# A message-passing layer on one core: loads between the parts of the tables, and gathers 8 to 13 that wait in half groups

## The chip, the cores and the metric

The kernel runs on one core of one Trainium2 chip. The metric is the device time in microseconds of one execution. Every time of a profile comes from one profiled execution and is counted from the start of its span, from the first to the last instruction.

## The reference, cut to what matters

A graph has 6250 nodes of 128 features and 100000 edges, sorted by destination. An edge's message is a small network of its source, its destination and four attributes; messages are summed by destination; a second network and two layer norms finish each node.

```python
src, dst = edge_index[0], edge_index[1]
msg_in = jnp.concatenate([node_features[src], node_features[dst], edge_features], axis=1)
h = jax.nn.silu(msg_in @ mW1 + mb1)
messages = h @ mW2 + mb2
aggregated = jax.ops.segment_sum(messages, dst, num_segments=N)
upd_in = jnp.concatenate([node_features, aggregated], axis=1)
u = jax.nn.silu(upd_in @ uW1 + ub1)
updated = u @ uW2 + ub2
return layer_norm(node_features + updated, ln_g, ln_b)
# and outside: x = layernorm(x + that)
```

Everything is float32.

## The kernel before, in words

**Tables.** The first layer is split by its inputs. For every node the kernel computes x times the source part of mW1 (`tab_a`) and x times the destination part plus the bias (`tab_b`) and stores both in HBM. This goes in seven `parts` of up to eight tiles of 128 nodes: `turn_x` transposes x on TensorE one part ahead, a product of 256 columns makes both tables at once, ScalarE copies one half, VectorE adds the bias to the other, and SyncE (SP) stores both (lines 377 to 405). The products use three PSUM buffers called `wide`.

**Groups.** The edges are worked in 98 groups of 1024, eight tiles of 128. For each group GpSimd (POOL) gathers eight tiles of rows by source index, one indirect DMA a tile (`fetch`, line 278). Groups 0 to 4 (`RAW = 5`) gather from x itself, because the table is not there yet, and are transposed later (`turn_rows` for groups 0 to 3, `turn_late` for group 4); from group 5 on they gather from `tab_a`. There are six gather buffers, so group g also waits until group g − 6 has been used.

**The loop over groups.** In iteration g: `load(g + 4)` brings the window of 96 rows of `tab_b` (`mv`, five buffers) that the group's sorted destinations fall into, the transposed attributes, and for every fourth group the list of near destinations; `hidden(g)` adds the gathered rows on VectorE and applies Silu on ScalarE; `products(g + 2)` makes on TensorE the part of the hidden layer that comes from destinations and attributes, out of a 0/1 matrix (`node_matrix`); `edge_matrix(g + 1)` makes the matrix for the sums; `by_nodes(g)` sums the messages' hidden rows into destinations on TensorE; `add(g − 2)` adds them to `acc`. Finished ranges of nodes go through `node_batch`, in pieces between the groups. For groups 0 to 4 `products` also multiplies the transposed gathered rows by the weights, so it holds twice as many matmuls as for later groups. A float32 product of 128 columns stands in the trace as two matmul records and two weight loads.

**What sets the order.** The order on SP, TensorE, VectorE and ScalarE is the order of the program. POOL's queue is ordered by a scheduler, which can put a tile that has to wait behind others of its own or the next group. `fetch(g, *after)` takes instructions of TensorE as extra dependencies: with one, tile 0 waits for it; with two, tile 0 waits for the first and tile 4 for the second. `begun[g]` is the first matmul of `products(g)`, `summing[g]` the first of the sums of g. The line in the code that names the reason reads "TensorE keeps up with the gathers". From group 14 on (`CLOSE`), group g waits in halves for `begun[g]` and `summing[g - 2]`; groups 5 to 13 wait as a whole for `begun[g - 5]`:

```python
        ahead = g + AHEAD
        if CLOSE <= ahead < NG:
            fetch(ahead, begun[ahead], summing[g])
        elif RAW <= ahead < NG:
            fetch(ahead, begun[ahead - 5])
```

Between the tables and the loop stand the loads that the first groups need (lines 406 to 414): the attribute rows of the weights into `mv`, the first chunk of attributes and its transposed rows in HBM (`attributes`, `attribute_rows`), the near destinations of groups 0 to 3 (`destinations`), fourteen window bases into registers of SP and VectorE (`load_bases`), and the four `turn_rows`.

Of the kernel before, what the change touches and what calls it, by code (L numbers as in the profile page):

```python
# [24 lines left out]
def kernel(  # L25
# [40 lines left out]
    nc = tc.nc  # L66
    N, H = x.shape
# [6 lines left out]
    NG = -(-E // GE)  # L74
    assert NG <= P
    W = 96
    NW = NP + W
    K1 = W + ED
    RB = 14
    AHEAD = 2  # L80
    CLOSE = 14
    LEAD = 4
    RAW = 5
# [14 lines left out]
    def groups(n, g):  # L98
        return [(i, min(g, n - i)) for i in range(0, n, g)]


    TURNED = 4
# [20 lines left out]
    def wide():  # L123
        return tables_ps.tile([P, G, P], F32, name="wide")
# [47 lines left out]
    mv = [consts.tile([K1, H], F32, name=f"mv{k}") for k in range(NM)]  # L172
# [102 lines left out]
    def tiles_of(g):  # L275
        return min(G, -(-(E - g * GE) // P))

    def fetch(g, *after):

        rows[g] = gath.tile([P, G, H], F32, name="ga")  # L280
        for i in range(tiles_of(g)):
            ins = nc.gpsimd.indirect_dma_start(  # L282
                out=rows[g][:, i, :],
                out_offset=None,
                in_=x if g < RAW else tab_a[:, :],
                in_offset=bass.IndirectOffsetOnAxis(
                    ap=src_i[:, g, i : i + 1] if g else src_0[:, i : i + 1], axis=0
                ),
            )
            part, at = divmod(i * len(after), G)  # L290
            if after and at == 0:
                tc.add_manual_dep(
                    ins.ins,
                    after[part].ins.name,
                    mybir.DependencyInfo(
                        mybir.DependencyClass.Sync, mybir.DependencyReason.DATA
                    ),
                    reason="TensorE keeps up with the gathers",
                )
# [8 lines left out]
    def attributes(c):  # L308
        t = turn.tile([EQ, EJ * ED], F32, name="ea_l")
        chunk = edge_attr[c * EC : (c + 1) * EC]  # L310
        nc.sync.dma_start(t, chunk.rearrange("(q j) d -> q (j d)", q=EQ))
        ea_l[c] = t

    def attribute_rows(c):
        t = turn.tile([EQ, ED, EJ], F32, name="ea_t")
        nc.scalar.copy(t, ea_l.pop(c).rearrange("q (j d) -> q d j", d=ED))
        rows = ea_d[:, c * EC : (c + 1) * EC]
        nc.sync.dma_start(rows.rearrange("d (q j) -> q d j", q=EQ), t)

    def destinations(g):  # L320

        n = min(NQ, NG - g)
        t = work.tile([W, NQ, GE], U8, name="near")
        flat = near_d[g : g + n].rearrange("(o g) e -> o (g e)", o=1)
        nc.sync.dma_start(
            t[:, :n].rearrange("w g e -> w (g e)"), flat.to_broadcast([W, n * GE])
        )
        for k in range(n):
            near[g + k] = t[:, k, :]
# [4 lines left out]
    def by_node(t):  # L334
        return t[:NP].rearrange("(i p) f -> p i f", p=P)
# [5 lines left out]
    def turn_x(i0, n):  # L341
        pt = wide()
        for i in range(n):
            ins = nc.tensor.transpose(pt[:, i, :], x_sb[:, i0 + i, :], ident)  # L344
        nc.scalar.copy(xT[:, i0 * P : (i0 + n) * P], pt[:, :n, :].rearrange("p i f -> p (i f)"))
        return ins

    def load_bases(g):
        _, vals = nc.values_load_multi_w_load_instructions(
            base_i[0:1, g : g + RB],  # L350
            engines=(ENG.SP, ENG.DVE),
            min_val=0,
            max_val=NP,
            skip_runtime_bounds_check_because=IN_RANGE,
        )
        for k, v in enumerate(vals):
            bases[g + k] = v
# [4 lines left out]
    def turn_rows(g):  # L362

        px = wide()
        for i in range(G):
            nc.tensor.transpose(px[:, i, :], rows[g][:, i, :], ident)
        nc.vector.tensor_copy(rows[g], px)
# [9 lines left out]
    for k, (i0, n) in enumerate(parts):  # L377
        if k + 1 < len(parts):
            turn_x(*parts[k + 1])

        tb = x_sb[:, i0 : i0 + n, :]
        ta = tpool.tile([P, G, H], F32, name="t", bufs=2)
        for j0, m in groups(n, G // 2):
            pm = wide().rearrange("p (i s) f -> p i s f", s=2)
            for j in range(m):
                cols = slice((i0 + j0 + j) * P, (i0 + j0 + j + 1) * P)
                ins = nc.tensor.matmul(pm[:, j], xT[:, cols], w1, start=True, stop=True)  # L387
            own = slice(j0, j0 + m)
            nc.scalar.copy(ta[:, own], pm[:, :m, 0, :])
            nc.vector.tensor_add(  # L390
                tb[:, own], pm[:, :m, 1, :], b1[:, None, :].to_broadcast([P, m, H])
            )
        nc.sync.dma_start(by_node(tab_a)[:, i0 : i0 + n, :], ta[:, :n])
        nc.sync.dma_start(by_node(tab_b)[:, i0 : i0 + n, :], tb)
        table.append(ins)
        if k == 1:
            fetch(2, *table)
        if k == 2:
            destination_lists()
        if k == 3:  # L400
            fetch(3, *table[2:])
        cols = slice(i0 * P, NW if i0 + n == NT else (i0 + n) * P)
        nc.vector.memset(acc[:, cols], 0.0)
        if k == 4:
            fetch(4, table[4])
    for t in mv:
        nc.sync.dma_start(t[W:], mW1[2 * H :])
    attributes(0)
    attribute_rows(0)
    destinations(0)  # L410
    load_bases(0)
    for g in range(TURNED):
        turn_rows(g)
    if E < NG * GE:
        pad = tpool.tile([ED, NG * GE - E], F32, name="pad")
# [6 lines left out]
    def rows_ps():  # L422
        return ps.tile([P, G, P], F32, name="pre")

    def node_y():
        return node_ps.tile([P, BT, H], F32, name="y")
# [173 lines left out]
    def edge_matrix(g):  # L600

        oh = work.tile([P, G, W], F32, name="oh", bufs=3)
        nc.vector.tensor_tensor(  # L603
            oh,
            w_row[:, None, :].to_broadcast([P, G, W]),
            rel[:, g, :, None].to_broadcast([P, G, W]),
            op=OP.is_equal,
        )
        return oh

    begun, summing = {}, {}

    def products(g):
        pre = rows_ps()
        st = stbuf[g % NST].rearrange("k (i c) -> k i c", i=G)
        for i in range(tiles_of(g)):
            ins = nc.tensor.matmul(pre[:, i, :], st[:, i, :], mv[g % NM], start=True, stop=g >= RAW)  # L617
            begun.setdefault(g, ins)
            if g < RAW:
                nc.tensor.matmul(  # L620
                    pre[:, i, :], rows[g][:, i, :], w1[:, 0, :], start=False, stop=True
                )
        return pre
# [26 lines left out]
    def by_nodes(g, h, oh):  # L650

        pt = degrees(g)
        sums(g, pt, h, oh, 0, tiles_of(g))
        return pt
# [13 lines left out]
        node_matrix(g)  # L668
    oh, h, pt, running = {0: edge_matrix(0)}, {}, {}, []
    pre = {g: products(g) for g in range(2)}  # L670
    for g in range(NG):
        if g == 3:
            load_weights()
        if g == 4:
            destination_checks(node_y())
        if g == 5:
            fuse_weights()
        for c in range(1, NC):
            if g == max(1, c * EC // GE - 10):
                attributes(c)  # L680
            if g == max(1, c * EC // GE - 10) + 1:
                attribute_rows(c)
        if g + LEAD < NG:
            load(g + LEAD)
        last = g >= NG - 1
        if not last:
            h[g] = hidden(g)
        if TURNED <= g + 2 < RAW:
            turn_late(g + 2)
        if g + 2 < NG:  # L690
            pre[g + 2] = products(g + 2)
        if g + MADE < NG:
            node_matrix(g + MADE)
        if g + 1 < NG:
            oh[g + 1] = edge_matrix(g + 1)
        if g - 2 in pt:
            add(g - 2, pt.pop(g - 2))
        if last:
            break
        pt[g] = by_nodes(g, h.pop(g), oh.pop(g))  # L700
        ahead = g + AHEAD
        if CLOSE <= ahead < NG:
            fetch(ahead, begun[ahead], summing[g])
        elif RAW <= ahead < NG:
            fetch(ahead, begun[ahead - 5])
        if g >= NG - 3:
            add(g - 1, pt.pop(g - 1))
        for i0, n, first in batches[:-1]:
            if g == (first if first >= NG - 3 else first + 1):
                running.append(node_batch(i0, n, *node_tiles(nodes, node_y)))  # L710
        for _ in range(2 if g >= NG - 6 else 1):
            advance(running)

    g = NG - 1
# [194 lines left out]
```

## Time and profile before

| what | us |
|---|---|
| median of 3 runs | 1210.3 (1208.65 to 1211.81) |
| the profiled execution | 1208.8 |
| its span | 1207.0 |
| POOL busy | 740.8 (61%) |
| TensorE matmuls busy | 735.1 (61%) |
| VectorE busy | 488.3 (40%) |
| ScalarE busy | 244.6 (20%) |
| mean busy share of the DMA engines, by slice | 0.6 to 0.7 at the start, 0.1 to 0.3 in the loop |
| mean granted TensorE clock | 0.678 |

No engine is busy all the time. The busy time of POOL is that of issuing gathers; their data move on the DMA engines. The idle time of an engine is put down in the profile to what released it: another engine's line, a DMA, "issue" where no wait ended just before, or "remote" where the release could not be matched to an instruction.

### The profile page before, as it was taken

What the parts mean: (1) busy time and instruction counts of PE and PEld (TensorE: products, weight loads), DVE (VectorE), ACT (ScalarE), POOL (GpSimd) and SP (SyncE); (2) the same over time, 40 slices, a digit from 0 to 9 for tenths busy, and PEclk for the clock granted to TensorE, in tenths of its full rate; (3) what the DMA queues carried; (4) which work ended last, traced back from release to release, by engine and by line L of the source; (5) the groups of instructions that cost most, each with busy time, mean ns of one, the idle gap of its engine ahead of it and who ended that gap; (6) DMA issues with size and microseconds to landing.
All of it is one profiled execution on the core that took longest, in us unless ns stands there. A gap on an engine that the chain in (4) does not pass through costs nothing.

```text
span 1207.0 us, 11413 instructions
## 1 busy us (share of the span) xinstructions
PE 735.1 (61%) x3655; PEld 656.4 (54%) x3655; DVE 488.3 (40%) x1023; ACT 244.6 (20%) x306; POOL 740.8 (61%) x790
## 2 busy tenths in 40 slices
PE   4655366855666576556556556655575665485673
PEld 3545366745555465456446445554565654474562
DVE  3460253634325325326326326326236235235343
ACT  1211012312103202112112103102112211211224
POOL 7536554466666666666666666666666666566660
PEclk9777766876657666766666776676676567666666
DMA  7653121323222313222222223222322222222220
GB/s 186 177 158 89 41 56 39 85 60 80 72 52 79 78 50 84 55 74 72 82 58 71 76 57 77 73 54 74 79 57 76 63 69 74 57 69 65 54 53 24
DMA packets 70221, 88.96 MB, mean 74 GB/s; under 512 B 20719, under 2 KB 51838, under 8 KB 70154
## 3 DMA queue, kind: packets, MB, share of 16 engines
q0 software_dynamic: 25024, 51.30, 17.3%
q1 hardware_dynamic: 40552, 34.96, 10.0%
q10 hardware_dynamic: 4578, 1.89, 0.6%
q8 instruction: 31, 0.51, 0.2%
q14 instruction: 36, 0.29, 0.1%
HBM read 76.71 MB, written 11.38 MB: 73 GB/s over the span
## 4 chain that ended last, share of the span: by engine, by line
issue 40%; POOL 27%; another core or an unknown queue 10%; DVE 9%; PE 9%; DMA 3%; ACT 1%; SPq 1%; DVEq 0%; POOLq 0%; ACTq 0%
POOL ga L282 27%; PE pt L645 2%; PE pre L617 2%; PE wide L387 2%; DVE oh L603 2%; DVE s L633 1%; DVE st L590 1%; DMA ga<-tab_a,src_i 1%; DVE st L482 1%; DMA x_sb<-in_x_dram 1%; DVE y L526 1%; PE wide L344 1%; DVE mv L483 0%; DMA w<-in_L_gnn_mW_dram 0%
## 5 line engine op out<-in xcount | busy, mean ns | idle before, releaser
L282 POOL DMA_INDIRECT ga<-tab_a,src_i x742 | 701.7, 946 | 412.9 <-issue 209.8
L617 PE MATMUL pre<-mv,st 100*128 100x128 f32 x1564 | 318.2, 366 | 189.8 <-issue 150.6
L645 PE MATMUL pt<-oh,h 128*128 128x96 f32 x1564 | 305.9, 349 | 209.2 <-issue 200.1
L645 PEld LDWEIGHTS pt<-oh,h 128*128 128x128 f32 x1564 | 286.0, 266 | 229.1 <-issue 220.7
L617 PEld LDWEIGHTS pre<-mv,st 100*128 100x128 f32 x1564 | 288.8, 274 | 212.6 <-issue 179.8
L633 DVE TENSOR_TENSOR s<-ga,pre 128x1024 f32<-128x1024 f32 x92 | 112.2, 1220 | 426.9 <-DMA ga<-tab_a,src_i 207.9
L634 ACT ACTIVATE h<-s 128x1024 f32<-128x1024 f32 x92 | 97.0, 1056 | 655.6 <-issue 367.3
L590 DVE TENSOR_SCALAR_CACHE_REDUCE st<-near,p_next 96x1024 f32<-96x1024 uint8 x98 | 124.2, 1269 | 6.2 <-DMA near<-near_d 6.0
L603 DVE TENSOR_TENSOR oh<-w_row,rel 128x768 f32<-128x768 f32 x98 | 93.1, 950 | 27.1 <-remote 24.0
L526 DVE TENSOR_TENSOR y<-y,xs 128x512 f32<-128x512 f32 (+2 forms) x13 | 8.4, 648 | 130.5 <-issue 110.0
L282 POOL DMA_INDIRECT ga<-in_x_dram,src_i x32 | 30.3, 947 | 17.4 <-issue 8.2
L634 ACT ACT_TABLE_LOAD x25 | 32.1, 1283 | 15.7 <-PE pre L620 13.8
L488 ACT ACT_TABLE_LOAD x26 | 33.4, 1283 | 3.6 <-DVE mv L483 3.1
L387 PE MATMUL wide<-w,xT 128*128 128x256 f32 x98 | 26.8, 432 | 10.7 <-DVE x_sb L390 8.0
L513 ACT ACTIVATE uT<-y,ub_col 128x512 f32<-128x512 f32 (+2 forms) x13 | 8.4, 645 | 116.8 <-remote 90.1
L387 PEld LDWEIGHTS wide<-w,xT 128*128 128x128 f32 x98 | 21.1, 222 | 15.0 <-DVE x_sb L390 8.6
L524 PEld LDWEIGHTS y<-u,uT 128*128 128x128 f32 x94 | 22.2, 318 | 9.0 <-issue 8.9
L524 PE MATMUL y<-u,uT 128*128 128x128 f32 x94 | 25.4, 419 | 0.0
L663 DVE TENSOR_TENSOR deg<-deg,pt 1x96 f32 x98 | 24.4, 249 | 1.0
L658 DVE TENSOR_TENSOR acc<-acc,pt 128x96 f32 x98 | 23.7, 242 | 1.8 <-PE pt L645 1.7
L483 DVE BATCH_NORM_AGGREGATE mv<-st 128x2 f32<-128x6 f32 x98 | 17.8, 182 | 13.1 <-remote 5.1
L620 PE MATMUL pre<-w,ga 128*128 128x128 f32 x80 | 19.8, 332 | 2.2 <-issue 2.2
(122 smaller groups left out, 368.3 us busy)
## 6 DMA issues: line engine op xcount, KB each, us to landing
ga<-tab_a,src_i POOLq DMA_INDIRECT x742
near<-near_d SPq DMA_DIRECT2D x24, 384.0 KB
mv<-tab_b SPq DMA_DIRECT2D x98, 48.0 KB
tab_a<-t SPq DMA_DIRECT2D x6, 512.0 KB
tab_b<-x_sb SPq DMA_DIRECT2D x6, 512.0 KB
xs<-in_x_dram SPq DMA_DIRECT2D x11, 256.0 KB
out_dram<-z SPq DMA_DIRECT2D x11, 256.0 KB
st<-ea_d SPq DMA_DIRECT2D x98, 16.0 KB
```

What stands on the lines that cost most here:

```text
L282: ins = nc.gpsimd.indirect_dma_start(out=rows[g][:, i, :], out_offset=None, in_=x if g < RAW else tab_a[:, :], in_offset=bass.IndirectOffs ...
L387: ins = nc.tensor.matmul(pm[:, j], xT[:, cols], w1, start=True, stop=True)
L488: nc.scalar.activation(r[:, :n], mv[:, :n, 1], AF.Sqrt, bias=eps)
L524: nc.tensor.matmul(y[:, i, :], by_p[:, :, i], u2, start=False, stop=i == n - 1)
L590: nc.vector.tensor_scalar(stbuf[g % NST][:W], near.pop(g), p_next, 0.0, op0=OP.is_equal, op1=OP.add, accum_out=deg_q[g // DQ % 2][:, g % D ...
L603: nc.vector.tensor_tensor(oh, w_row[:, None, :].to_broadcast([P, G, W]), rel[:, g, :, None].to_broadcast([P, G, W]), op=OP.is_equal,)
L617: ins = nc.tensor.matmul(pre[:, i, :], st[:, i, :], mv[g % NM], start=True, stop=g >= RAW)
L633: nc.vector.tensor_add(s[:, :n], ga[:, :n], ps[:, :n])
L634: nc.scalar.activation(h[:, :n], s[:, :n], AF.Silu)
L645: ins = nc.tensor.matmul(pt[:, :W], h[:, i, :], oh[:, i, :], start=i == 0, stop=i == tiles_of(g) - 1)
L658: nc.vector.tensor_add(at, at, pt[:, :W])
L663: nc.vector.tensor_add(at, at, pt[row, W:])
```

## The change

Three things are done. The loads named above, and the turns of groups 0 and 1, are put between the parts of the tables: the attributes after part 0, the weights' rows after part 1, the transposed attribute rows and the first turn after part 3, the near destinations, the bases and the second turn after part 4. The gathers of groups 5 to 7 are issued before the loop and lose their wait for products. Groups 8 to 13 are then issued in every second iteration, from iteration 1 to 11, and each waits in two halves: group 8 for products 2 and 3, group 9 for 4 and 5, and so on to group 13 for 12 and 13. From group 14 on the waits are the same.

```diff
@@ -77,7 +77,6 @@
     RB = 14
-    AHEAD = 2
     CLOSE = 14
@@ -393,23 +392,26 @@
         table.append(ins)
+        if k == 0:
+            attributes(0)
         if k == 1:
             fetch(2, *table)
+            for t in mv:
+                nc.sync.dma_start(t[W:], mW1[2 * H :])
         if k == 2:
             destination_lists()
         if k == 3:
             fetch(3, *table[2:])
+            attribute_rows(0)
+            turn_rows(0)
         cols = slice(i0 * P, NW if i0 + n == NT else (i0 + n) * P)
         nc.vector.memset(acc[:, cols], 0.0)
         if k == 4:
             fetch(4, table[4])
-    for t in mv:
-        nc.sync.dma_start(t[W:], mW1[2 * H :])
-    attributes(0)
-    attribute_rows(0)
-    destinations(0)
-    load_bases(0)
-    for g in range(TURNED):
+            destinations(0)
+            load_bases(0)
+            turn_rows(1)
+    for g in range(2, TURNED):
         turn_rows(g)
@@ -668,6 +670,9 @@
     pre = {g: products(g) for g in range(2)}
+
+    for g in range(RAW, 8):
+        fetch(g)
     for g in range(NG):
@@ -698,11 +703,11 @@
         pt[g] = by_nodes(g, h.pop(g), oh.pop(g))
-        ahead = g + AHEAD
-        if CLOSE <= ahead < NG:
-            fetch(ahead, begun[ahead], summing[g])
-        elif RAW <= ahead < NG:
-            fetch(ahead, begun[ahead - 5])
+        if CLOSE <= g + 2 < NG:
+            fetch(g + 2, begun[g + 2], summing[g])
+        elif g % 2:
+            at = g // 2 + 8
+            fetch(at, begun[g + 1], begun[g + 2])
         if g >= NG - 3:
```

## The prediction

> **What bounds the kernel now.** First the page: POOL, which issues the gathers, has the costliest group.
>
> ```profile
> span 1207.0 us, 11413 instructions
> ...
> L282 POOL DMA_INDIRECT ga<-tab_a,src_i x742 | 701.7, 946 | 412.9 <-issue 209.8
> ```
>
> One gather is busy for 946 ns, and the timeline shows 0.30 us before the next one of an undisturbed run: 1.25 us each, 978 us for all 782. The other 229 us of the span are what must be understood. The waits of POOL (us in total, times, longest) say where they are:
>
> ```profile
> POOL ga L282 <- issue: 220.2, 680, 11.8
> POOL ga L282 <- remote: 138.7, 55, 4.0
> POOL ga L282 <- PE pre L617: 37.2, 8, 20.0
> POOL ga L282 <- DMA mv<-in_L_gnn_mW_dram: 10.5, 1, 10.5
> ```
>
> Most of "issue" is the 0.30 us. "Remote" is a wait of 2.5 to 4 us about every 16 gathers; by the built program nearly all of these are waits for TensorE, whose release was not matched. The long ones lie at the start. The timeline of POOL (start, us, what, idle before it), from the first gather of the new table to where the steady pattern begins:
>
> ```profile
> 71.33 0.94 POOL L282 DMA_INDIRECT ga<-tab_a,src_i  x1 [10.53 <-DMA mv<-in_L_gnn_mW_dram]
> ...
> 83.37 0.94 POOL L282 DMA_INDIRECT ga<-tab_a,src_i  x1 [3.61 <-PE pre L617]
> 88.23 0.94 POOL L282 DMA_INDIRECT ga<-tab_a,src_i  x1 [3.92 <-PE pre L617]
> ...
> 161.06 0.94 POOL L282 DMA_INDIRECT ga<-tab_a,src_i  x1 [11.76 <-issue]
> ...
> 221.19 0.94 POOL L282 DMA_INDIRECT ga<-tab_a,src_i  x1 [20.00 <-PE pre L617]
> ```
>
> The last line is the mark of this prediction, M: the first tile of group 14, which waits for the product of group 14. Before it lie 78 gathers of the table: 97.5 us of work in 149.9 us, so 52 us of pauses. After it POOL issues 664 gathers, at 1.44 us each, and the tail follows.
>
> Why is TensorE late? The stretches (busy us and number of PE, PEld, DVE, ACT, POOL; clock, DMA share, GB/s) show it working in fits:
>
> ```profile
> 82.00:96.00 14.00, 13.68 (x106) 13.71 (x107) 7.02 (x11) 4.31 (x4) 6.89 (x8) 0.85 0.38 101
> 96.00:111.00 15.00, 4.72 (x18) 3.94 (x18) 0.00 (x0) 0.10 (x1) 9.15 (x10) 0.63 0.35 77
> ...
> 119.00:131.00 12.00, 0.00 (x0) 0.00 (x0) 0.00 (x0) 0.33 (x1) 8.13 (x9) 0.69 0.22 56
> ...
> 174.00:184.00 10.00, 3.41 (x10) 2.40 (x11) 0.35 (x1) 0.28 (x2) 5.19 (x6) 0.71 0.17 44
> ...
> 204.00:221.00 17.00, 15.07 (x104) 14.70 (x104) 15.88 (x32) 10.53 (x11) 0.00 (x0) 0.75 0.25 68
> ```
>
> While POOL gathers without a break, TensorE runs fast for 90 to 140 records (weight loads and matmuls together, mostly 105 to 127), then drops to about one matmul a microsecond, until POOL pauses. Every slow stretch ends when POOL has stood still for about 2 us. Counted in the timeline, a pause of 2.0 us or more brings the fast pace back; pauses of 1.0 and 1.1 us (at 787.5 and 1111.2) did not. So POOL's pauses feed TensorE, and TensorE's lateness makes the pauses.
>
> **What the Trainium skill says.** "SBUF — State Buffer", Who interferes with whom, has PE share no port with GpSimd and only the DVE and GpSimd pair contend; so ports don't explain the slow stretches, which the trace shows all the same (18 matmuls in 15 us). "Runtime: NRT & Kernel Launch", Instruction fetch mechanics, calls fetching autonomous and mostly hidden, in blocks of 256 instructions; the 105 to 127 records fit no such block. I name no mechanism and use the measured pattern.
>
> **The change, part by part.** From 82.2 to 221.2 TensorE issued 532 matmuls in 139.0 us. Slow were 96–111, 119–131, 144–150, 174–184 and 195–204: 52 us with 50 matmuls. Outside them 482 matmuls took 87 us, 5.5 per us.
>
> *Loads moved (SP, ACT).* No transfer is added. Five loads of mv rows (1.79 us of issue at 68.96), attributes, their rows, near and the load of bases leave the stretch after the tables. In SP's queue they now stand ahead of later table stores, which could wait behind them. SP's gaps between stores are 3 to 9 us there, so I take nothing for the loads; the load of bases takes 1.55 us on SP and its engine DVE waits too. The moved ACT copy (1.08 us) falls in a gap of 2.3 us. If SP had no gap, the five loads and near would cost some 2.3 us.
>
> *First nodes turned earlier.* Two of the four turns (8 transposes, 1.1 us; one DVE copy, 1.16 us) go between the parts. DVE then holds 2.3 us of copies and about 1.8 us of base loading more before the last adds, in a part where it was busy for 5.0 of 7.3 us; TensorE's last products wait for the second copy's buffer. I take 1.9 us for the last store of tab_a: gathers begin at 73.2 instead of 71.33. Bounds: 0 and 4.1 us.
>
> *Start of the products.* Before: the pad is stored late (76.79, behind near and bases), near lands at about 80.2, first product 82.3. After: the last two copies end near 71.8, pad issues at 72.3, lands 2.9 us later as before (76.79 to 79.70), the st load goes at 75.2, and 2.6 us later (79.70 to 82.33 before) the first product starts: 77.8, so 4.5 us earlier.
>
> *New waits.* Gathers 5 to 7 lose the wait for products; 6 and 7 still wait for the buffers of groups 0 and 1 (six buffers). By the built order, from M on POOL's queue is identical. Before M, halves of groups 8 to 13 wait for products 2 to 13, two groups of TensorE (128 records) per eight gathers (10 us). The walk, with 108 fast records per pause of 2 us or more and 1.4 records per us when they are used up:
> - 73.2–83: group 5. Product 0 (64 records, 5.6 us) ends at 83.4; a pause of 0.5 us refills nothing.
> - 83.7–93.4: group 6. Product 1 runs dry at 86.5; slow for 10 us. Pause 3 us.
> - 96.5–116.2: groups 7 and 8. Slow from 104, 14 us. Pause 4 us.
> - From 120.5: waits at each half group. Pauses at about 129, 140 (6 us more behind the destination checks on DVE), 158, 171, 186 and 199, each ending about 2 us after the refill; slow for 12 us in all.
>
> Slow time is then 36 us by the walk; I take 34. With t for the whole ramp, 5.5 (t − 34) + 34 = 532 gives t = 124.5, so M lies at 77.8 + 124.5 = 202.3; POOL's own work needs 73.2 + 97.5 = 170.7 and 32 us of pauses remain, six to eight of 3 to 5 us, which agrees. M gains 18.9 us. All behind the gathers (DVE adds, sums, node batches) waits on the same queue; the cover of the moved waits is the lead of gathers, which at M is again one to two groups in both kernels.
>
> *Sum.* 1207.0 − 18.9 = 1188.1 of span. The profiled execution was 1208.8, 1.8 above its span: 1189.9. The median of runs, 1210.3, is 1.5 above that: 1191.4, call it 1192.
>
> **Rivals.**
> 1. *Only the earlier start counts.* Slow time stays at 52 us and TensorE's 139 us move as they are: M at 216.8, 4.4 us gained, 1206. For it: M waits for TensorE, whatever POOL does. Against: before, five unbroken bursts of 10 to 20 us made the slow time; after, only two of 20 us remain.
> 2. *Slower: the ramp takes the steady pace.* From 221.2 to 1165 TensorE did 2833 matmuls in 943.8 us, 3.0 per us, with POOL pausing only when caught. If freeing groups 5 to 7 and splitting the rest leave only pauses too short to refill, the ramp goes that way: 532 / 3.0 = 177 us, M at 255, 34 us lost, 1244. Halfway (3.4 per us) M is at 234, 1223. It decides against the change below 532 / 143.4 = 3.71 per us. For it: the 20.00 us pause, in which TensorE did 104 matmuls, goes. Against: two groups per eight gathers hold POOL back twice as often as the steady one.
> 3. *Bound by POOL.* Every wait finds TensorE ready after the least pause: 170.7 plus seven pauses of 2.5 us, M at 188, 33 us gained, 1177.
>
> **How the numbers follow.** Forecast 0.55, ending at 1180 to 1200 by slow time of 20 to 44 us; rival 1 has 0.15, rival 2 0.20, rival 3 0.10. A measurement tells about 0.3%, 3.6 us, from no change. Rival 1 lies at its edge: 0.06 of it counts as faster, 0.08 as same, 0.01 as slower. Faster 0.71, same 0.08, slower 0.21. The range must leave out 2 in 10: from 1176 (rival 3 in) to 1221 (the milder half of rival 2). The tables' 0 to 4.1 us and the loads' 2.3 us lie within it.
>
> **What would show it.** First gather from tab_a at 72 to 75; first product near 78, not 82; the eighth gather of group 5 no longer behind a pause; pauses of 3 to 5 us between 120 and 200 and none of 12 or 20; M near 202; from M to the end 986 us as before; "remote" waits about the same in number or a few more. Wrong: a first product after 82 (the tables were delayed by more than the loads saved), slow stretches above 52 us before M, or more than 3 us change behind M, where I claim nothing changes.

## The result, and the profile after

The changed kernel takes 1194.2 us (median of 4 runs, 1194.1 to 1194.9) against 1209.5 for the kernel before: a ratio of 0.987, interval 0.9855 to 0.989. The forecast was 1192. The kernel before takes either about 1026 or about 1210 us and stays with one of them through a sitting, and on one and the same chip both were seen; the result, and the prediction, belong to the second.

The page of the changed kernel shows the gathers costing as much work as before (701.8 us) and having 19 us less idle time ahead of them (393.7, not 412.9):

```profile
span 1192.3 us, 11417 instructions
...
L281 POOL DMA_INDIRECT ga<-tab_a,src_i x742 | 701.8, 946 | 393.7 <-issue 194.4
```

POOL's waits (us in total, times, longest) say which ones went. The 20.0 us wait for a product is gone, and the longest wait for one is now 5.4; "remote", the steady wait, is 132.1 us for 138.7. The wait for the table (the first line of the timeline below) is 11.5 us:

```profile
POOL ga L281 <- issue: 204.5, 670, 0.5
POOL ga L281 <- remote: 132.1, 48, 4.0
POOL ga L281 <- PE pre L619: 26.4, 10, 5.4
```

The timeline of POOL, from the first gather of the new table to M, the first tile of group 14 (start, us, what, idle before it):

```profile
74.81 0.94 POOL L281 DMA_INDIRECT ga<-tab_a,src_i  x1 [11.47 <-DMA tab_a<-t]
...
86.52 0.94 POOL L281 DMA_INDIRECT ga<-tab_a,src_i  x1 [2.03 <-remote]
...
131.85 0.94 POOL L281 DMA_INDIRECT ga<-tab_a,src_i  x1 [5.33 <-PE pre L619]
...
156.37 0.94 POOL L281 DMA_INDIRECT ga<-tab_a,src_i  x1 [5.47 <-DVE s L635]
...
204.54 0.94 POOL L281 DMA_INDIRECT ga<-tab_a,src_i  x1 [1.94 <-remote]
```

M lies at 204.54 instead of 221.19. The two pauses of 11.8 and 20.0 us ahead of it have become many of 2 to 5.5. The stretches of this ramp (busy us and number of PE, PEld, DVE, ACT, POOL; clock, DMA share, GB/s), from the first product to M, then the three in which TensorE does little, then everything behind M up to the last gathers:

```profile
77.10:204.50 127.40, 87.00 (x539) 81.16 (x540) 52.21 (x112) 25.72 (x33) 71.70 (x76) 0.73 0.27 72
96.00:109.00 13.00, 4.35 (x15) 3.03 (x13) 0.00 (x0) 0.00 (x0) 7.75 (x9) 0.62 0.29 76
115.00:129.00 14.00, 0.33 (x4) 0.09 (x1) 0.00 (x0) 1.02 (x1) 8.78 (x10) 0.67 0.23 57
142.00:148.00 6.00, 0.00 (x0) 0.00 (x0) 1.90 (x3) 0.00 (x0) 1.90 (x3) 0.63 0.13 33
204.50:1165.00 960.50, 581.96 (x2890) 521.81 (x2890) 389.79 (x820) 195.19 (x237) 628.20 (x664) 0.67 0.26 67
```

Slow time is 33 us (13 + 14 + 6) with 19 matmuls; it was 52 us with 50. From 156 on POOL pauses about every eight gathers and TensorE shows no long slow stretch. From M to the end it is 987.8 us, against 985.8 before.

Only the first of the three is TensorE at a slow pace: there its records come one by one, often 0.70 us apart (a matmul at 107.01, a weight load at 107.71, a matmul at 108.41). From 115 on it waits for VectorE, which has to copy four transposes before TensorE can go on, and that copy starts 14.0 us after their end (114.73 + 0.60):

```profile
114.73 0.60 PE L372 MATMUL y<-ident,ga 128*128 128x128 f32 x4
129.29 0.69 DVE L373 COPY ga<-y 128x512 f32<-128x512 f32 x1 [44.42 <-remote]
130.04 1.11 PE L372 MATMUL y<-ident,ga 128*128 128x128 f32 x4 [14.71 <-DVE ga L373]
```

The semaphore update that lets the copy go stands in the trace at 129.27. The ends of matmuls are modelled, so whether the transposes or only their signal came late is open. The third stretch is of the same kind: VectorE's destination checks begin at 146.10, 4.6 us after the matmul whose result they read (141.07 + 0.46), and TensorE waits for them. The kernel before has both at the same places (the copy at 132.37, 13.6 us after the transposes). So what comes late while POOL gathers is not TensorE's pace alone; it is also the handing over from TensorE to VectorE.

### The profile page after: what moved, and what is told of

It reads as the page before. It is cut to its first block, busy times and chain, and to the rows that moved or that the text cites. A ratio compares the mean times of both kernels' runs of the same rounds, so it can differ in the third digit from the quotient of the medians.

```text
span 1192.3 us, 11417 instructions
## 1 busy us (share of the span) xinstructions
PE 723.3 (61%) x3655; PEld 646.4 (54%) x3655; DVE 488.3 (41%) x1023; ACT 244.9 (21%) x306; POOL 740.9 (62%) x790
## 4 chain that ended last, share of the span: by engine, by line
issue 39%; POOL 25%; PE 16%; another core or an unknown queue 6%; DVE 5%; DMA 1%; DVEq 1%; ACT 1%; SPq 0%; POOLq 0%; ACTq 0%
POOL ga L281 25%; PE pre L619 7%; PE pt L647 6%; DVEq L635 1%; DVE oh L605 1%; DMA ga<-tab_a,src_i 1%; DVE s L635 1%; DVE st L484 1%; PE y L526 1%; DVE y L528 1%; PE y L517 0%; PE y L510 0%; PE y L511 0%; PE y L512 0%
## 5 line engine op out<-in xcount | busy, mean ns | idle before, releaser
L281 POOL DMA_INDIRECT ga<-tab_a,src_i x742 | 701.8, 946 | 393.7 <-issue 194.4
L619 PE MATMUL pre<-mv,st 100*128 100x128 f32 x1564 | 315.7, 364 | 195.8 <-issue 141.7
L647 PE MATMUL pt<-oh,h 128*128 128x96 f32 x1564 | 292.2, 341 | 188.5 <-issue 177.5
L647 PEld LDWEIGHTS pt<-oh,h 128*128 128x128 f32 x1564 | 276.1, 259 | 205.9 <-issue 196.8
```

What stands on the lines that cost most here:

```text
L281: ins = nc.gpsimd.indirect_dma_start(out=rows[g][:, i, :], out_offset=None, in_=x if g < RAW else tab_a[:, :], in_offset=bass.IndirectOffs ...
L647: ins = nc.tensor.matmul(pt[:, :W], h[:, i, :], oh[:, i, :], start=i == 0, stop=i == tiles_of(g) - 1)
```

## The experiments

My theory: TensorE keeps its pace only while POOL pauses now and then (in the 1210 us condition, as it turned out), so the half groups that hold POOL back shorten the ramp, and the moved loads start it sooner. Rival 1: only the sooner start counts. A further question came with the first four: what are the slow stretches, if a chip can run without them?

**1. Loads and turns moved, waits as before.** Against the changed kernel:

```diff
-    for g in range(RAW, 8):
-        fetch(g)
...
-        if CLOSE <= g + 2 < NG:
-            fetch(g + 2, begun[g + 2], summing[g])
-        elif g % 2:
-            at = g // 2 + 8
-            fetch(at, begun[g + 1], begun[g + 2])
+        ahead = g + AHEAD
+        if CLOSE <= ahead < NG:
+            fetch(ahead, begun[ahead], summing[g])
+        elif RAW <= ahead < NG:
+            fetch(ahead, begun[ahead - 5])
```

> The kernel before with the loads and the first two turns moved between the parts of the tables, and nothing else: groups 5 to 13 wait as before. My theory (the moved loads give the earlier start, the new waits shorten the slow time of TensorE): first product at 77 as in the changed kernel (5 us before the old 82.3), the 20 us pause ahead of group 14 stays (15 to 22 us), the first tile of group 14 at 216 plus or minus 4 instead of 221.2, time about 1205 (1201 to 1209). Rival 1 (only the start counts) has the whole gain here: first tile of group 14 at 204 to 206, time 1193 to 1196. A rival by which an early start is eaten up by POOL running unbroken through groups 5 and 6: first tile of group 14 at 221 or later, time 1209 or more.

Measured: 1022.7 against 1026.0 for the kernel before beside it, 0.996 (0.994 to 0.9975). Every number expected was for a condition that was not there: M came at 157.2, not 216.

**2. The new waits alone.** Against the changed kernel:

```diff
-        if k == 0:
-            attributes(0)
         if k == 1:
             fetch(2, *table)
-            for t in mv:
-                nc.sync.dma_start(t[W:], mW1[2 * H :])
...
-            attribute_rows(0)
-            turn_rows(0)
...
             fetch(4, table[4])
-            destinations(0)
-            load_bases(0)
-            turn_rows(1)
-    for g in range(2, TURNED):
+    for t in mv:
+        nc.sync.dma_start(t[W:], mW1[2 * H :])
+    attributes(0)
+    attribute_rows(0)
+    destinations(0)
+    load_bases(0)
+    for g in range(TURNED):
         turn_rows(g)
```

> The changed kernel with loads and turns put back behind the tables; groups 5 to 7 without a wait and 8 to 13 in half groups, as in the change. My theory: first gather of the new table at 71.3, first product at 82.3 as in the kernel before, a ramp as long as the changed kernel's (127 us), the first tile of group 14 at 208 to 210, no pause of 10 us or more ahead of it, time 1197 to 1200. Rival 1: slow time is as before, first tile of group 14 at 219 to 223, time 1207 to 1211. Rival by which the two parts need each other: no gain here and none in the other half, 1207 or more in both.

Measured: 1025.3, 0.9996 (0.9988 to 1.0003): in this condition the waits alone are worth nothing. POOL's timeline of this kernel says why. The first gather of the table is 3.4 to 5.8 us earlier than where the loads are moved (57.4 to 59.8 in 1 and 3 to 7), but group 6 then waits for a buffer, which the late first product (66.4) holds:

```profile
54.06 0.94 POOL L281 DMA_INDIRECT ga<-tab_a,src_i  x1 [0.77 <-DMA mv<-in_L_gnn_mW_dram]
...
73.08 0.94 POOL L281 DMA_INDIRECT ga<-tab_a,src_i  x1 [9.33 <-PE pre L619]
```

**3. Groups 8 to 13 released as before.** Groups 5 to 7 stay free, the loads stay moved:

```diff
-        elif g % 2:
-            at = g // 2 + 8
-            fetch(at, begun[g + 1], begun[g + 2])
+        elif g >= 6:
+            fetch(g + 2, begun[g - 3])
```

> The changed kernel in which groups 8 to 13 wait as they did before, whole groups on the product five groups earlier; groups 5 to 7 stay free and the loads stay moved. POOL may run further ahead. My theory (POOL must be held back early for TensorE to keep its pace): bursts of 16 and more gathers, a pause of 12 to 22 us ahead of group 14, its first tile at 212 to 220, time 1202 to 1210. Rival (what gained was the free start of groups 5 to 7 and the earlier products; holding POOL back does nothing): first tile of group 14 at 203 to 206, time 1193 to 1196.

Measured: 1022.5, 0.9965 (0.9953 to 0.9977).

**4. Whole groups.**

```diff
-            at = g // 2 + 8
-            fetch(at, begun[g + 1], begun[g + 2])
+            fetch(g // 2 + 8, begun[g + 2])
```

> The changed kernel in which groups 8 to 13 wait once, for the second of the two products (8 for product 3, 13 for product 13), not in halves. My theory: the half that waited for the earlier product comes later; pauses grow to 5 to 7 us and there are six of them, TensorE is fast nearly throughout and the slow time before group 14 falls below 30 us; the first tile of group 14 at 202 to 209, time 1192 to 1199. Rival (the halves themselves are what gains, since whole groups make bursts too long): first tile of group 14 at 212 or later, time above 1202.

Measured: 1023.1, 0.9966 (0.9951 to 0.9981). Like 3 it tells nothing on the waits here, because no wait of groups 8 to 13 stops POOL. Whether halves or whole groups matter in the other condition stays open.

**5, 6 and 7. The kernels of 1 and 3 and the changed kernel, once more.**

> The kernel with only the loads and turns moved, once more, since on the chip of the first four experiments the kernel before took 1026 us, not 1210: POOL issued 742 gathers there without one pause and TensorE never fell to its slow pace. What I hold now: there are two conditions, one with slow stretches of TensorE (the kernel before at 1208 to 1212) and one without (1024 to 1030), and my forecast is about the first. If the kernel before takes about 1210 here: the 20 us pause ahead of group 14 stays (15 to 22 us), first tile of group 14 at 216 plus or minus 4, 1205 (1201 to 1209) by my theory; 1193 to 1196 by rival 1 (only the start counts). If it takes about 1026: 1022 to 1024 again.

> The changed kernel with groups 8 to 13 waiting as before (whole groups, on the product five groups earlier), once more. If the kernel before takes about 1210 here: by my theory (POOL must be held back for TensorE to keep its pace) bursts of 16 and more gathers, a pause of 12 to 22 us ahead of group 14, its first tile at 212 to 220, 1202 to 1210; by the rival (holding back does nothing) 1193 to 1196. If about 1026: 1022 to 1023 again.

> The changed kernel itself beside the two others. If the kernel before takes about 1210 here: 1193 to 1196. If about 1026: POOL's gathers set the time, so what counts is where they start and whether a wait of the change holds them up. The start can come no more than 1 us earlier than in the kernel with only the loads moved (1022.7), and the half groups that wait for products 2 to 13 may stop POOL for 0 to 10 us in all: 1022 to 1033; by the reading that TensorE is always ahead there, 1022 to 1024.

Measured, beside a kernel before of 1025.4: loads alone 1021.1 (0.9951 to 0.9975), old release 1021.8 (0.9958 to 0.9978), the changed kernel 1022.6, 0.998 (0.9965 to 0.9988). So in this condition the change gives a quarter of a per cent, and the loads alone give all of it. The changed kernel's page, its waits and its first 20 us of products show what is different from the 1192.3 us profile of the same program:

```profile
span 1019.3 us, 11417 instructions
...
L281 POOL DMA_INDIRECT ga<-tab_a,src_i x742 | 703.6, 948 | 231.3 <-issue 189.2
L619 PE MATMUL pre<-mv,st 100*128 100x128 f32 x1564 | 315.6, 379 | 301.4 <-DVE s L635 277.8
```

```profile
POOL ga L281 <- issue: 200.2, 657, 0.3
```

```profile
61.00:81.00 20.00, 20.00 (x165) 19.81 (x165) 6.21 (x9) 6.37 (x6) 15.09 (x16) 0.92 0.57 139
```

A gather still takes 948 ns and 0.3 us to the next one, but POOL issues all 742 of the table without one pause, from 58.58 on. TensorE does 165 matmuls in 20 us beside 16 unbroken gathers, where it did 18 in 15 us in the other condition. And its idle time ahead of `pre` is now a wait for VectorE, which waits for gathered rows; in the 1192.3 us profile that group's largest part waits for nothing that the profile shows:

```profile
L619 PE MATMUL pre<-mv,st 100*128 100x128 f32 x1564 | 315.7, 364 | 195.8 <-issue 141.7
```

This last difference lies in part in the records. The five traces of the 1210 us condition hold 4832 to 5077 semaphore updates, the eight of experiments 1 to 8 hold 17970 to 18004, for programs of nearly the same instructions. A wait whose end was not recorded stands as "issue" or "remote". The longest "issue" ahead of `pre` in the 1192.3 us profile, 8.69 us, ends at 285.35, just after an addition on VectorE (to 285.30); ScalarE, which reads that very sum, starts at 285.33 and is put down to "issue" too:

```profile
284.08 1.22 DVE L635 TENSOR_TENSOR s<-ga,pre 128x1024 f32<-128x1024 f32 x1 [9.79 <-issue]
285.33 1.06 ACT L636 ACTIVATE h<-s 128x1024 f32<-128x1024 f32 x1 [8.22 <-issue]
```

Of the idle time ahead of `pre` in that profile some 107 us end within 0.3 us of such an addition; the profile puts down 38.3 to it. What does not hang on these records is the count of matmuls, and the copy that came 14.0 us late above. Here it starts as its transposes end (81.05):

```profile
81.08 0.69 DVE L373 COPY ga<-y 128x512 f32<-128x512 f32 x1 [12.02 <-PE y L372]
```

So unbroken gathers alone don't slow TensorE or the handing over: something else has to be there, and it isn't in the program.

**8. Tables first.** A version against both kernels, from what 2 and 7 show: the sooner start of the table (54.1) and the sooner first product (61) together. Against the changed kernel:

```diff
-    gath = edges.enter_context(tc.tile_pool(name="gath", bufs=6))
+    gath = edges.enter_context(tc.tile_pool(name="gath", bufs=7))
...
         if k == 0:
             attributes(0)
+            if E < NG * GE:
+                pad = tpool.tile([ED, NG * GE - E], F32, name="pad")
+                nc.vector.memset(pad, 0.0)
+                nc.sync.dma_start(ea_d[:, E:], pad)
...
             fetch(4, table[4])
-            destinations(0)
-            load_bases(0)
-            turn_rows(1)
-    for g in range(2, TURNED):
+    destinations(0)
+    load_bases(0)
+    for g in range(1, TURNED):
         turn_rows(g)
-    if E < NG * GE:
-        pad = tpool.tile([ED, NG * GE - E], F32, name="pad")
-        nc.vector.memset(pad, 0.0)
-        nc.sync.dma_start(ea_d[:, E:], pad)
```

> A version of the changed kernel meant to beat both: the near load, the load of bases and the turn of group 1 go back behind the tables, the pad is stored in the first part, and the gathers have seven buffers, not six. Without slow stretches (the kernel before at 1024 to 1030) POOL issues all gathers at 1.25 us each, so the time follows the first gather of the new table that no later wait interrupts: 58.6 in the changed kernel, 54.1 with the loads behind the tables. If those three steps are what delays the tables: first such gather at 54 to 55.5, no pause of more than 1 us behind it, time 1017 to 1020 against 1022.6 for the changed kernel. If the loads of the first part or the first turn delay the tables, or group 0's product comes after 64 and group 7 must wait for it: 1021 to 1024. With slow stretches (the kernel before at about 1210): tables at 71.5, but group 14 waits for TensorE anyway, so 1190 to 1197.

Measured: 1019.8 against 1026.1 beside it, 0.994 (0.9923 to 0.9957), where the changed kernel had 0.9965 to 0.9988: better than both in this condition. Its first gather of the table comes 2.2 us sooner than the changed kernel's 58.58, though not at the 54 to 55.5 expected, and no pause follows:

```profile
56.36 0.94 POOL L281 DMA_INDIRECT ga<-tab_a,src_i  x1 [3.27 <-DMA tab_b<-x_sb]
```

Which of its steps gains is not told apart. The start of the table in one execution says little, since executions of the same code differ in it by 1.3 and 1.6 us here (59.82 and 58.48 in 1 and 5, 57.43 and 59.04 in 3 and 6). In the 1210 us condition the version was not run. That it would gain there too is only argued.

**9. A load on the DMA engines.** Do transfers held up by other traffic make the slow stretches? The copies go to a place that nothing reads:

```diff
+        if g >= 8:
+            nc.scalar.dma_start(spare[g % 4][:, :], x[:4096])
         pt[g] = by_nodes(g, h.pop(g), oh.pop(g))
```

> The changed kernel with a copy of 2 MB from x to a spare place in DRAM on ACT's queue in each group from 8 on (90 copies, 180 MB read and as much written): does a load on the DMA engines and on memory bring the slow stretches of TensorE? If the slow stretches come from transfers held up by other traffic: TensorE falls to about one matmul per us within bursts of gathers, POOL shows pauses of 3 to 5 us again, time 1100 to 1250. If the slow stretches have nothing to do with the load on the DMA engines: a gather stays at 0.94 + 0.30 us, no POOL pause of 2 us or more apart from transfers that are late for DVE, TensorE's matmuls stay as dense, time 1022 to 1060.

Measured: 1081.5, ratio 1.056 (1.0526 to 1.0596); slower than the 1022 to 1060 of the second answer, but of its kind. Traffic rose from 87 to 255 GB/s, and what came of it are waits for gathered rows, of POOL (66.9 us, longest 4.8) and, through VectorE, of TensorE:

```profile
L620 PE MATMUL pre<-mv,st 100*128 100x128 f32 x1564 | 324.8, 387 | 352.6 <-DVE s L636 321.8
```

The 141.7 us of "issue" ahead of `pre` don't appear. A load of this kind does not bring the slow stretches.

**10. The kernel before, with a profile.**

> The kernel before, unchanged, with a profile on the chips of the experiments. If it takes 1024 to 1028 here: one unbroken run of POOL from about 62 to 64 (group 5 waits for product 0), no pause of 2 us or more behind it, no stretch in which TensorE does one matmul per us while its inputs are there, and the 0.94 + 0.30 us of a gather as ever. That would say that the slow stretches aren't made by the gathers alone. If it takes about 1210: the pauses and slow stretches of the first profile at the same places within 3 us.

Measured: 1211.0 beside 1213.7 for the same kernel, on the chip that had carried experiments 5 to 7 at 1025. The other condition was back, and with it the pauses at their places: 11.76 us ahead of 162.96, and M at 221.68:

```profile
221.68 0.94 POOL L282 DMA_INDIRECT ga<-tab_a,src_i  x1 [18.58 <-PE pre L617]
```

**11. The new waits alone, again,** the kernel of 2, beside 10.

> The new waits alone, once more. If the kernel before takes about 1026 here: 1024 to 1026, no gain, since POOL only exchanges the wait for product 0 ahead of group 5 for one of 9 us ahead of group 6. If it takes about 1210: first gather of the new table at 71.3, first product at 82.3, first tile of group 14 at 208 to 210, 1197 to 1200 by my theory (the waits shorten the slow time); 1207 to 1211 by rival 1 (only the start counts).

Measured: 1201.9 (1197.5 to 1206.9) against 1213.7, ratio 0.990 (0.9846 to 0.995). The profiled execution took 1202.4. POOL's timeline of it, and the whole ramp:

```profile
77.12 0.94 POOL L281 DMA_INDIRECT ga<-tab_a,src_i  x1 [10.24 <-DMA mv<-in_L_gnn_mW_dram]
...
93.90 0.94 POOL L281 DMA_INDIRECT ga<-tab_a,src_i  x1 [7.10 <-PE pre L619]
...
164.76 0.94 POOL L281 DMA_INDIRECT ga<-tab_a,src_i  x1 [5.47 <-DVE s L632]
...
211.86 0.94 POOL L281 DMA_INDIRECT ga<-tab_a,src_i  x1 [1.90 <-PE pt L639]
```

```profile
88.20:211.90 123.70, 84.61 (x544) 79.74 (x545) 53.14 (x115) 25.79 (x33) 66.07 (x71) 0.75 0.26 71
```

The tables ended 6 us later in this execution than in 10 (77.12 against 71.19) though their code is the same, so the first product came at 88.2, not 82.3, and M at 211.9, not 208 to 210. The ramp took 123.7 us where the kernel before takes 139: my theory, 15 us by the waits alone, with no help from a sooner start. Rival 1, at 1207 to 1211, falls: the interval puts the kernel 0.5% or more below the one before, and no start came sooner.

**12. Old release, a third time,** the kernel of 3.

> The changed kernel with groups 8 to 13 waiting as before (whole groups, on the product five groups earlier), a third time. The new waits alone took TensorE's ramp from the first product to the first tile of group 14 from 139 us to 124 us where the kernel before takes about 1210. Which part of them does it? If the kernel before takes about 1210 here: by my theory (holding POOL back in half groups, for products 2 to 13) bursts of 14 and more gathers stay up to group 14, a pause of 12 to 22 us ahead of it, ramp of 134 to 142 us, first tile of group 14 at 212 to 220, 1202 to 1210. By the rival (the freed groups 5 to 7 do it, with the fewer pauses in the first 40 us) ramp of 124 to 130 us, 1193 to 1197. If about 1026: 1021 to 1023 again, and the question stays open.

Measured: 1223.7 against 1224.6 beside it (all a little slower on this chip), ratio 0.998 (0.9959 to 0.9999). The timeline has both long pauses back; the stretches are the ramp and three of the slow ones:

```profile
161.65 0.94 POOL L281 DMA_INDIRECT ga<-tab_a,src_i  x1 [12.50 <-issue]
...
222.12 0.94 POOL L281 DMA_INDIRECT ga<-tab_a,src_i  x1 [20.11 <-PE pre L619]
```

```profile
77.50:222.10 144.60, 88.13 (x531) 83.29 (x532) 51.24 (x109) 24.37 (x31) 71.72 (x76) 0.70 0.24 64
95.00:110.00 15.00, 4.62 (x13) 3.39 (x14) 0.00 (x0) 0.14 (x1) 8.95 (x10) 0.56 0.29 67
117.00:132.00 15.00, 0.00 (x0) 0.00 (x0) 0.27 (x1) 1.02 (x1) 8.78 (x10) 0.62 0.20 53
145.00:153.00 8.00, 0.00 (x0) 0.00 (x0) 2.07 (x3) 0.00 (x0) 3.23 (x4) 0.69 0.15 41
```

The first product is as early as in the changed kernel (77.5), and M as late as in the one before: the five microseconds of the start are gone in a ramp of 144.6, a little above the 134 to 142 expected. Freeing groups 5 to 7 is not by itself what gains; holding POOL back in groups 8 to 13 is. The slow stretches come back with the old release, two of these three without one matmul: there TensorE waits for VectorE as in the changed kernel, whose copy now starts at 131.73, 15.0 us after the transposes. Behind M it takes 1000.2 us, 11 to 14 more than in the other four profiles of this condition; neither the kernel before nor the changed one has a profile on this chip. Whether it is the halves or the later products they wait for, 12 doesn't tell apart.

## Why the prediction was right, by its own steps

The same sum with what was measured: M at 204.5, plus 987.8 behind it, is the span of 1192.3; 1.9 us more is the median of 1194.2. The forecast had 202.3, 985.8 and 3.3.

- **Tables: mis-sized.** The first gather of the table came at 74.81, not 73.2: in this pair of traces the loads and turns took 3.5 us of the tables, within the bounds of 0 to 4.1 but not the 1.9 taken. One pair does not settle it, since the end of the tables moved by 6 us between 10 and 11. In the other condition it was 3.4 to 5.8 us. That it cost nothing in the changed kernel's ramp, since the first product came later still, is argued, not shown; in the other condition 8, which takes part of it back among other things, was faster.
- **First product: right.** 77.1 for 77.8, 5.2 us sooner than before.
- **The walk: right in kind, with one pause wrong.** After group 5 I had a pause of 0.5 us that refills nothing; it was 2.03, and the next slow stretch began at 96, not 86.5. The other pauses ended at 109.4, 131.9, 136.1, 150.0, 168.9, 180.8 and 192.7, and VectorE's destination checks show as the 5.47 us ahead of 156.37.
- **Slow time: 33 us for 34, but emptier.** I let one matmul through per slow microsecond, 34 in all; there were 19. The formula with the measured terms, (539 − 19) / 5.5 + 33, gives 127.5, and the trace has 127.4. Fifteen matmuls less in the slow time and seven more in the ramp are four us at 5.5 per us; one us less slow time takes some back. That is the 2.9 us by which the ramp is longer than forecast. That the sum of slow time fits is in part luck: the walk had 10 us from 86.5, 14 from 104 and 12 at the half groups, and the trace has none from 86.5, 13 from 96, 14 from 115 and 6 from 142. And the last two, 20 of the 33 us with four matmuls, are waits for VectorE, which starts late; the prediction read such stretches of the kernel before as TensorE's slow pace.
- **Behind M: unchanged, as claimed.** 987.8 against 985.8, and the second profile of the kernel before has 988.7 (1210.4 − 221.7).
- **Rivals.** Rival 1 is refuted by 11 and 12 where the prediction was made, and is what happens in the other condition. There the first product came sooner by 4.3 us when the loads moved (66.4 in 2, 62.1 in 1), and the time with them by 3.3 to 4.3. Rival 2 did not come: pauses of 2.0 to 2.3 us were enough to refill, at 86.5, 180.8 and 192.7. Rival 3, bound by POOL, is the other condition too, further than I had it: no pause at all in the changed kernel.

What the prediction lacked is the condition. "POOL's pauses feed TensorE" was read out of one profile; the pattern comes back in every profile of the 1210 us kind, but it is no property of the program; in the 1026 us kind the same change gives 2.8 us. The prediction's 0.55 for its forecast had no case for that.

By how much the loads gain in the 1210 us condition is not settled: the whole change has 0.9855 to 0.989, the waits alone 0.9846 to 0.995. Loads alone were never run there. From 12 one would argue that they gain almost nothing without the new waits.

## What to carry to other kernels

When an engine idles and the profile calls it "issue" or "remote", look first whether a result that it needs had come just before, since the record of that can be missing. Where none had, or the result itself came late, ask what another engine was doing at that moment, and try to hold that one back in small portions rather than once for long: here pauses of 2 to 5.5 us, 32 us in all up to M (129.7 us less 97.5 of gathers), took the place of 52 us that had a 12 and a 20 among them. Take the pattern from one profile as a property of that profile until a second one, from another sitting, shows it too; profile the unchanged kernel again beside the experiments. Before loads are moved ahead of a store, see what the store's end releases: here some 3.5 us of delay were the price of a product 5 us sooner, and in the other condition a version that avoids about half of the delay was faster still (8).

## What the runs showed of the hardware

- One program, two conditions: 1025.4 and 1211.0 us for the kernel before on the same chip at different times, with the same gathers (946 to 948 ns each, 0.3 us between). In the slower one TensorE falls to about one matmul per us (15 in 13 us in the changed kernel) while POOL gathers without a break, and in all five traces one copy on VectorE starts 12.1 to 15.0 us after the transposes that it reads, where it takes 0.04 us in experiments 1 to 8. Both recover when POOL stops; pauses of 2.0 to 2.3 us were enough for TensorE. The condition shows before the ramp too: with the tables' code unchanged the first gather of the table came at 54.1 in 2 and at 71.2 in 10.
- What makes the condition is open. A load on the DMA engines and memory by this core did not bring it (255 GB/s in 9, no such stretch), and the number of instruction transfers does not differ. The Trainium skill, "Runtime: NRT & Kernel Launch", Instruction fetch mechanics, has blocks of 16 KiB; the pages of both conditions list 31 transfers of an instruction queue with 0.51 MB together, which agrees in size, and is the same in both. Other users of the chip or the placement in memory weren't tried. A further suspect is the recording of the traces: it keeps less than a third of the semaphore updates in the slower condition. Whether recording slows the engines there, or loses records for the same reason for which they are slow, no run here tells, since none was set beside an execution without a trace.
- The end of the tables moves by 6 us between executions of the same code (71.19 and 77.12 in 10 and 11).
